# A four-layer graph network on one core: the sort's transposes get a PSUM bank of their own, the second batch's layers have two

## The chip, the cores and the metric

The kernel runs on one core of a Trainium2 chip. The metric is the device time of one execution in microseconds (us), and of several executions the median. A profile is one more execution with the hardware profiler on: it has a span from the first to the last instruction, and a time of its own that is a little longer than the span. The engines are TensorE (PE), VectorE (DVE), ScalarE (ACT), GpSimd (POOL) and SyncE (SP), which issues most of the DMA transfers. ACT issues some transfers too.

## The reference

Sixteen graphs of 1024 nodes and 64 channels go through four layers, each of them x = x + layer(relu(layernorm(x))). Layer 0 drops some edges of each node, sorts the values of the remaining neighbours in each channel, and takes three quantiles:

```
h = jnp.maximum(_layernorm(x, axis=-1), 0.0)
x = x + _L0_gnn_ref(h, adj, nodemask, ...)       # below
...
vals = jnp.where(nd[..., None], x[:, None, :, :], jnp.inf)
s = jnp.sort(vals, axis=2)
...
for tau, w in zip(TAUS, WTS):
    agg = agg + w * (v_lo + frac * (v_hi - v_lo))
out = x + agg
y = relu(out @ W1 + b1) @ W2 + b2
```

Layer 1 multiplies the adjacency matrix by a small network's output and feeds a gated unit. Layer 2 multiplies it by h again. Layer 3 is an attention over the columns of the adjacency matrix with a softmax. All three need the adjacency matrix, transposed, as a matmul operand.

## The kernel before

**Pairs.** The batches are worked off two at a time, `pairs = B // 2`, so there are eight pairs. What is done for one pair:

- `sort_begin` (L692): loads x of the two batches, normalises it, stores h, and transposes it by eight matmuls (L714) into a tile `cur` with one row for each of 2 x 64 channels. ACT copies the result out of PSUM (L717).
- `sort_pair` (L720): a bitonic network of 55 steps on DVE sorts each channel's 1024 values (L729, L736, L737). Each four steps, the comparisons' results go to DRAM (`m_d`, L740, on SP's queue). Then the 55 steps are undone on a code (L753 to L760), which gives each node its rank code. ACT turns the code into f32 (`cf`, L794), eight matmuls transpose it back (L799), ACT copies it out (L800), and it goes to DRAM as `y_d` (L802).
- `prepare` / `neighbours` (L805): loads the adjacency matrix (`a`, L819), transposes it into `a_d` for the layers (L831, L833), and makes the thinned matrix `ndT` (L825, L854 to L881). A last group of matmuls counts the neighbours (L885), read by DVE (L892).
- `weights` and `select` (L907, L1028): `weights` loads `y_d` into `node` and makes the pieces `wt` from it on DVE (L916, L921). `select` multiplies them by `ndT` (L1045) and picks the quantiles (L1055 to L1160). `extras` (L1251) handles the nodes that did not fit.
- `layers` (L1324): the dense part of layer 0 and layers 1 to 3 of one batch. The matmuls write tiles of one PSUM pool, `bank()` (L1339). `adj_block` loads `a_d` on SP's queue (L1402).

**Order.** The loop at L1566 has, for pair pr: select for pr, extras for pr, then the layers of both batches of pr, and beside them `prepare(pr + 1)`, `sort_pair(pr + 1)` and `sort_begin(pr + 2)`. Nobody writes out the order of an engine's instructions. When the program is built, a list scheduler with its own estimates of durations places each instruction as early as its operands and a free buffer allow, and earlier program text goes first. So the steps of a sort fill DVE's gaps wherever their data is ready. At run time each engine follows the order that was made, waits included. Buffers of one name in a pool are handed out in turn.

**PSUM.** A tile of 512 f32 per partition is one bank. In the layers' stage the pool `nbp` has two banks under one name, `pk`, the pool `lb0` three for the first batch of the pair and `lb1` three for the second. That is all eight. `nbp`'s two serve `prepare` (L829, L865, L882) and the sort's two sets of transposes (L712, L797) alike. `select` uses all eight banks itself (`sp`, `sc`), `extras` six beside `nbp`. The sort's SBUF rows (`row4`, L689) have three buffers and live through the whole kernel.

Of the kernel before, what the change touches and what calls it, by code (L numbers as in the profile page):

```python
# [9 lines left out]
F32 = mybir.dt.float32  # L10
# [10 lines left out]
PSUM = bass.MemoryType.PSUM  # L21
DRAM = bass.MemoryType.DRAM

P = 128
# [18 lines left out]
def gnn_stack(ctx, tc, x, adj, nodemask, w, out):  # L43
# [613 lines left out]
    def norm(pool, big, xt, g, name):  # L657

        st = pool.tile([P, g, 6], F32, name=f"{name}_st")
        mv = pool.tile([P, g, 2], F32, name=f"{name}_mv")  # L660
        for t in range(g):
            nc.vector.bn_stats(st[:, t, :], xt[:, t, :])
        for t in range(g):
            nc.vector.bn_aggr(mv[:, t, :], st[:, t, :])
        sd = pool.tile([P, g], F32, name=f"{name}_sd")
        nc.scalar.activation(sd, mv[:, :, 1], AF.Sqrt, bias=eps, scale=1.0)
        rs = pool.tile([P, g], F32, name=f"{name}_rs")
        nc.vector.reciprocal(rs, sd)
        d = big()
        nc.vector.tensor_sub(d, xt, mv[:, :, 0:1].to_broadcast([P, g, C]))  # L670
        h = big()
        nc.vector.scalar_tensor_tensor(
            h, d, 0.0, rs.rearrange("p (g o) -> p g o", o=1).to_broadcast([P, g, C]), op0=ALU.max, op1=ALU.mult
        )
        return h
# [13 lines left out]
    def row4():  # L689
        return so.tile([P, N], F32, name="s4", bufs=3)  # L690

    def sort_begin(pr, nbp):  # L692

        def rows():
            return row4().rearrange("p (g c) -> p g c", c=C)

        xt = rows()
        x4 = xt.rearrange("p (t b) c -> p t b c", b=2)
        for b in range(2):
            nc.sync.dma_start(x4[:, :, b, :], x[pr * 2 + b].rearrange("(t p) c -> p t c", p=P))  # L700
        h = norm(so, rows, xt, NT * 2, "so")
        h4 = h.rearrange("p (t b) c -> p t b c", b=2)
        for b in range(2):
            nc.sync.dma_start(h_d[pr * 2 + b], h4[:, :, b, :])
        more_ = so.tile([P, N], U16, name="code").bitcast(BF16)
        nc.scalar.activation(more_, h.rearrange("p g c -> p (g c)"), AF.Sign)
        more_ = more_.rearrange("p (t b c) -> p t b c", b=2, c=C)
        for b in range(2):
            nc.sync.dma_start(p_d[pr * 2 + b], more_[:, :, b, :])
        cur = row4()  # L710
        for q in range(0, NT, 4):
            ph = nbp.tile([P, 4, P], F32, name="pk")  # L712
            for t in range(4):
                nc.tensor.transpose(  # L714
                    ph[:, t, :], h[:, 2 * (q + t) : 2 * (q + t) + 2, :].rearrange("p b c -> p (b c)"), ident
                )
            nc.scalar.copy(cur[:, q * P : (q + 4) * P], ph.rearrange("p t n -> p (t n)"))  # L717
        return cur

    def sort_pair(pr, cur, nbp):  # L720

        nxt = row4()
        groups = range(0, len(steps), GROUP)
        for k0 in groups:
            swapped = so.tile([P, GROUP, N // 2], U16, name="swapped", bufs=2)
            for k, (size, j) in enumerate(steps[k0 : k0 + GROUP]):
# [11 lines left out]
                cur, nxt = nxt, cur  # L738
# [55 lines left out]
        nc.scalar.mul(cf, code, -4.0)  # L794
        cn = row4().bitcast(F16)[:, :N].rearrange("p (t k) -> p t k", k=P)
        for q in range(0, NT, 4):
            pc = nbp.tile([P, 4, P], F32, name="pk")  # L797
            for t in range(4):
                nc.tensor.transpose(pc[:, t, :], cf[:, (q + t) * P : (q + t + 1) * P], ident)  # L799
            nc.scalar.copy(cn[:, q : q + 4, :], pc)  # L800
# [106 lines left out]
    def weights(b, sb, behind):  # L907

        node = sb.tile([P, NT, 4, C], F16, name="node")
        nc.sync.dma_start(node[:, :, 0, :], y_d[b])
        positive = sb.tile([P, NT, C], BF16, name="positive", bufs=2)
        nc.sync.dma_start(positive, p_d[b])
        for k in range(1, 4):
            nc.vector.tensor_scalar_add(node[:, :, k, :], node[:, :, 0, :], 4.0 * CODE * k)  # L916
        wt = {}
        for g in PIECES:
            wt[g] = sb.tile([P, NT, 8, C], F8, name="wt", bufs=len(PIECES) + 2)
            for k in range(0, 8, 4):  # L920
                nc.vector.tensor_scalar(  # L921
                    wt[g][:, :, k : k + 4, :].bitcast(U8), node, 4.0 * (25 + CODE * (8 * g + k)), 4.0 * 26,
                    op0=ALU.add, op1=ALU.min,
                )
        order = ExitStack()
        rows = w_d[b * C : (b + 1) * C]
        for part, d_, w0, n in ((0, 4, 0, 32), (1, 4, 40, 32), (2, 16, 32, 8)):
            src = rows.rearrange("(q d) w e -> d w q e", d=d_)
            to = vtab[:, part].rearrange("p (q d e) -> p q d e", d=d_, e=24)
            for d in range(d_):  # L930
                if behind is not None:
                    order.enter_context(tc.issue_after(behind))
                    behind = None
                nc.sync.dma_start(to[d : d_ * n : d_, :, d, :], src[d, w0 : w0 + n])
        order.close()
        return wt, positive
# [603 lines left out]
    def prepare(pr, nb, nbp):  # L1540

        made = []
        for i in range(2):
            made.append((
                ndp.tile([P, NT, N], F8, name=f"ndT{i}"), ndp.tile([P, NT, 10], F32, name=f"row10{i}"),
                ndp.tile([P, NT, 3], F32, name=f"qb{i}"),
                ndp.tile([P, NT], F32, name=f"qz{i}"),
            ))
            neighbours(pr * 2 + i, *made[i], nb, nbp)
        return made  # L1550

    def side_pools():
        return (
            tc.tile_pool(reuse_waits="tile", name="nb", bufs=1),
            tc.tile_pool(reuse_waits="tile", name="nbp", bufs=2, space=PSUM),
        )

    pairs = B // 2
    nb_, nbp_ = side_pools()
    with nb_ as nb, nbp_ as nbp:  # L1560
        sort_pair(0, sort_begin(0, nbp), nbp)
        made = prepare(0, nb, nbp)
        if pairs > 1:
            cur = sort_begin(1, nbp)
    taken = None
    for pr in range(pairs):  # L1566
        with tc.tile_pool(reuse_waits="tile", name="keep", bufs=1) as keep:
            aggs = [keep.tile([P, NT, C], F32, name=f"agg{i}") for i in range(2)]
            kept = {
                "flag": [keep.tile([P, NT], U16, name=f"flag{i}") for i in range(2)],  # L1570
                "vx": keep.tile([P, 9], F32, name="vx"),
            }
            with tc.tile_pool(reuse_waits="tile", name="kn", bufs=1) as kn:
                with (
                    tc.tile_pool(reuse_waits="tile", name="sy", bufs=2) as sy,
                    tc.tile_pool(reuse_waits="tile", name="sw", bufs=1) as sw,
                    tc.tile_pool(reuse_waits="tile", name="sg", bufs=2) as sg,
                    tc.tile_pool(reuse_waits="tile", name="sp", bufs=2, space=PSUM) as sp,
                    tc.tile_pool(reuse_waits="tile", name="sc", bufs=2, space=PSUM) as sc,
                ):  # L1580
                    for i in range(2):
                        wt, positive = weights(pr * 2 + i, kn, None if i else taken)
                        select(pr * 2 + i, i, wt, positive, *made[i], aggs[i], kept, sw, sg, sy, sc, sp)
            nb_, nbp_ = side_pools()
            with nb_ as nb, nbp_ as nbp:
                with tc.tile_pool(reuse_waits="tile", name="xs", bufs=1) as xs, tc.tile_pool(reuse_waits="tile", name="xp", bufs=1, space=PSUM) as xp:
                    taken = extras(pr, kept, aggs, xs, xp)
                with (
                    tc.tile_pool(reuse_waits="tile", name="ly0", bufs=1) as ly0,
                    tc.tile_pool(reuse_waits="tile", name="ly1", bufs=1) as ly1,  # L1590
                    tc.tile_pool(reuse_waits="tile", name="lb0", bufs=3, space=PSUM) as lb0,
                    tc.tile_pool(reuse_waits="tile", name="lb1", bufs=3, space=PSUM) as lb1,
                ):
                    for i, (ly, lb) in enumerate(((ly0, lb0), (ly1, lb1))):
                        layers(pr * 2 + i, (pr * 2 + i) % 4, aggs[i], ly, lb)
                    if pr + 1 < pairs:
                        made = prepare(pr + 1, nb, nbp)
                        sort_pair(pr + 1, cur, nbp)
                    if pr + 2 < pairs:
                        cur = sort_begin(pr + 2, nbp)  # L1600
    sorting.close()


# [1 line left out]
    with tc.tile_pool(name="fl", bufs=1) as fl, tc.tile_pool(name="flp", bufs=1, space=PSUM) as flp:  # L1605
        pr = flp.tile([P, P], F32, name="pr")
# [41 lines left out]
```

## Time and profile before

| what | us |
|---|---|
| median of 3 runs (lowest, highest) | 6534.98 (6533.89, 6546.8) |
| the profiled execution, its own time | 6547.95 |
| the profiled execution, its span | 6546.1 |
| select of pair 1, in the profile | 1213.1 to 1674.6 |
| extras of pair 1 | 1674.6 to 1764 |
| layers of pair 1, with what runs beside them | 1764 to 1982.6 |
| select of pair 7, the last | 5828.2 to 6260.7 |
| extras of pair 7 | 6260.7 to 6325.8 |
| layers of pair 7, with nothing beside them | 6325.8 to 6536.3 |

A window of the profile gives, for each engine, the time in which it was busy and the number of its instructions. In a timeline a line is the start, the duration, the engine, the line of the kernel, the operation, what it writes and reads, and in brackets how long the engine had been idle before it and what ended that.

### The profile page before, as it was taken

What the parts mean: (1) busy time and instruction counts of PE and PEld (TensorE: products, weight loads), DVE (VectorE), ACT (ScalarE), POOL (GpSimd) and SP (SyncE); (2) the same over time, 40 slices, a digit from 0 to 9 for tenths busy, and PEclk for the clock granted to TensorE, in tenths of its full rate; (3) what the DMA queues carried; (4) which work ended last, traced back from release to release, by engine and by line L of the source; (5) the groups of instructions that cost most, each with busy time, mean ns of one, the idle gap of its engine ahead of it and who ended that gap; (6) DMA issues with size and microseconds to landing.
All of it is one profiled execution on the core that took longest, in us unless ns stands there. A gap on an engine that the chain in (4) does not pass through costs nothing.

```text
span 6546.1 us, 112888 instructions
## 1 busy us (share of the span) xinstructions
PE 4538.7 (69%) x45010; PEld 2819.2 (43%) x45010; DVE 5301.1 (81%) x13031; ACT 3545.5 (54%) x4348; POOL 137.5 (2%) x234
## 2 busy tenths in 40 slices
PE   0167858777577776778577775777767876777856
PEld 0145544355434544355443554344543544435532
DVE  7759985999769996899959998599977999586645
ACT  0165655556456556565555565555555655555623
POOL 0000000000000000000000000000000000000000
PEclk9978868788688887888788897888878888888967
DMA  1320135211451124401352114611155013520024
GB/s 56 110 72 33 57 106 177 70 42 49 137 176 39 50 89 141 128 35 51 92 187 75 39 52 118 188 48 51 51 157 150 33 59 89 176 70 16 8 69 126
DMA packets 525639, 568.14 MB, mean 87 GB/s; under 512 B 265004, under 2 KB 414894, under 8 KB 525102
## 3 DMA queue, kind: packets, MB, share of 16 engines
q1 hardware_dynamic: 381472, 476.43, 24.1%
q10 hardware_dynamic: 142862, 82.31, 4.1%
q8 instruction: 355, 5.82, 0.4%
q0 software_dynamic: 768, 2.10, 0.2%
q14 instruction: 182, 1.49, 0.1%
HBM read 376.95 MB, written 183.76 MB: 86 GB/s over the span
## 4 chain that ended last, share of the span: by engine, by line
PE 44%; DVE 23%; ACT 18%; DMA 11%; issue 4%; ACTq 0%; SPq 0%; POOL 0%; DVEq 0%; POOLq 0%
PE comb L1045 17%; PE cand L1148 6%; ACT sign L1103 6%; DMA adjT<-a_d 4%; PE comb L1101 4%; PE bank L1409 4%; DVE y L1119 3%; ACT y L1055 2%; PE comb L1236 2%; DMA a<-in_adj_dram 2%; PE pk L875 2%; DVE att L1519 2%; DVE adjT L1513 2%; DVE cand L1156 2%; DMA a_d<-at 1%
## 5 line engine op out<-in xcount | busy, mean ns | idle before, releaser
L1045 PE MATMUL comb<-wt,ndT 128*128 128x512 fp8e5 x6144 | 1518.2, 404 | 60.3 <-DVE top L1516 29.3
L1055 ACT ACTIVATE y<-comb,qb 128x1024 int16<-128x1024 f32 (+1 forms) x640 | 629.9, 1025 | 954.4 <-PE comb L1045 954.3
L1045 PEld LDWEIGHTS <-ndT 128*128 128x128 fp8e5 x6144 | 617.7, 103 | 804.3 <-issue 207.6
L1119 DVE TENSOR_TENSOR y<-y 128x512 uint16<-128x512 uint16 (+5 forms) x896 | 703.9, 790 | 66.5 <-PE comb L1101 50.8
L1148 PE MATMUL cand<-vtab,sign 128*128 128x48 f16 (+1 forms) x18432 | 680.6, 192 | 71.9 <-DVE agg L1018 29.0
L1148 PEld LDWEIGHTS <-sign 128*128 128x128 fp8e5 x18432 | 648.1, 97 | 143.6 <-issue 51.7
L1101 PE MATMUL comb<-ident_b,y 128*128 128x128 bf16 x4608 | 392.1, 255 | 436.2 <-ACT sign L1103 382.9
L1103 ACT ACTIVATE sign<-comb,half 128x2048 fp8e5<-128x2048 int16 (+1 forms) x384 | 591.6, 1541 | 124.1 <-PE comb L1101 112.1
L1103 ACT ACTIVATE sign<-comb,lower 128x2048 fp8e5<-128x2048 int16 (+1 forms) x384 | 590.9, 1539 | 0.0
L1156 DVE COPY_PREDICATED cand<-w_f,cand 128x256 f32<-128x256 uint16 (+1 forms) x1536 | 529.5, 376 | 70.7 <-PE cand L1148 69.1
L1101 PEld LDWEIGHTS <-y 128*128 128x128 bf16 x4608 | 357.9, 115 | 460.2 <-issue 454.0
L825 DVE TENSOR_TENSOR_SCAN cum<-ni 128x1024 f16<-128x1024 fp8e5 x128 | 292.9, 2294 | 149.3 <-ACT sq L854 131.1
L1409 PE MATMUL bank<-adjT,nd 128*64 128x512 f32 x1024 | 309.2, 662 | 97.0 <-DMA adjT<-a_d 91.7
L833 ACT COPY at<-pk 128x512 f32<-128x512 f32 x256 | 146.7, 586 | 334.5 <-DMA a_d<-at 167.6
L1409 PE MATMUL bank<-att,hs 128*64 128x512 f32 x512 | 206.9, 893 | 165.7 <-ACT hs L1524 164.8
L875 PE MATMUL pk<-ident_b,ni 128*128 128x128 bf16 x1024 | 217.8, 239 | 145.5 <-ACT at L833 80.0
L729 DVE TENSOR_TENSOR swapped<-s 128x512 uint16<-128x512 f32 x440 | 302.0, 686 | 12.2 <-DMA m_d<-swapped 3.9
L736 DVE TENSOR_TENSOR s<-s 128x512 f32<-128x512 f32 (+2 forms) x440 | 288.5, 656 | 0.0
L921 DVE TENSOR_SCALAR wt<-node 128x2048 uint8<-128x2048 f16 x224 | 267.6, 1216 | 25.8 <-PE comb L1236 25.7
L737 DVE TENSOR_TENSOR s<-s 128x512 f32<-128x512 f32 (+2 forms) x440 | 288.4, 655 | 0.0
L875 PE MATMUL pk<-minus_b,rem 128*128 128x128 bf16 x1024 | 219.3, 242 | 88.3 <-ACT rem L856 88.3
L760 DVE TENSOR_TENSOR code<-code,xo 128x1024 uint16<-128x1024 uint16 x360 | 264.2, 734 | 4.6
(300 smaller groups left out, 8065.3 us busy)
## 6 DMA issues: line engine op xcount, KB each, us to landing
adjT<-a_d SPq DMA_DIRECT2D x384, 512.0 KB
a<-in_adj_dram SPq DMA_DIRECT2D x128, 512.0 KB
a_d<-at ACTq DMA_DIRECT2D x256, 256.0 KB
m_d<-swapped SPq DMA_DIRECT2D x104, 512.0 KB
swapped<-m_d SPq DMA_DIRECT2D x104, 512.0 KB
n_d<-nat SPq DMA_DIRECT2D x128, 128.0 KB
x_d<-xr SPq DMA_DIRECT2D x48, 256.0 KB
comb_x<-x_d ACTq DMA_DIRECT2D x24, 512.0 KB
```

Source lines behind the costliest of these rows:

```text
L729: nc.vector.tensor_tensor(side(swapped[:, k, :], j), hi, lo, op=ALU.is_gt)
L736: nc.vector.tensor_tensor(to_lo, lo, hi, op=ALU.max)
L825: nc.vector.tensor_tensor_scan(cum[:, t - t0, :], ni[:, t, :], wide[:, t, pad - 1 : pad - 1 + N], 0.0, op0=ALU.add, op1=ALU.add)
L875: nc.tensor.matmul(pk[:, n % 4, :], lhs, rhs, start=(n % 4 == 0 and m == 0), stop=(m == len(terms) - 1 and last),)
L1045: nc.tensor.matmul(pw[:, e, :], ndT[:, j, t * P : (t + 1) * P], piece[:, j].rearrange("p w c -> p (w c)"), start=(j == 0), stop=(j == NT - 1),
L1055: nc.scalar.activation(y[:, 0, chunks, at : at + words_ * d_].rearrange("p q (w d) -> p q w d", d=d_), by_word[:, : words_ * C].rearrange( ...
L1101: nc.tensor.transpose(pt[:, q - q0, :], y[:, 0, q, :].bitcast(BF16), ident_b)
L1103: nc.scalar.activation(signs[tl][s][:, q0:q1, :], pt.bitcast(I16), AF.Sign, bias=before[s], scale=-1.0, saturate=False,)
L1119: nc.vector.tensor_tensor(v[:, :, :, :n], v[:, :, :, :n], v[:, :, :, n : 2 * n], op=ALU.max)
L1148: nc.tensor.matmul(cand[:, e, at : at + 12 * d_].rearrange("p (d l) -> p d l", l=12), signs[tl][sec][:, chunk, :], tab[:, q, :, half_ * 12 ...
L1156: nc.vector.copy_predicated(v[:, :, :, dst : dst + k], mk.to_broadcast([P, 2, C // 2, k]), v[:, :, :, frm : frm + k])
L1409: nc.tensor.matmul(po[to : to + C, :], lhs, rhs[:, f * HALF : (f + 1) * HALF], start=(j == 0), stop=(j == NT - 1))
```

## The change

The sort's transposes no longer take tiles of `nbp`. They take them from a new pool `sop` with one bank, and the name of the tile is `ps`. In the loop that bank is opened beside the layers' pools, so it exists from the end of `extras` to the end of the layers. `lb1` gives up one of its three banks for it. Before the loop `sop` stands beside `nbp`. No instruction is added or taken away.

```
-    def sort_begin(pr, nbp):
+    def sort_begin(pr, sop):
...
-            ph = nbp.tile([P, 4, P], F32, name="pk")
+            ph = sop.tile([P, 4, P], F32, name="ps")
...
-    def sort_pair(pr, cur, nbp):
+    def sort_pair(pr, cur, sop):
...
-            pc = nbp.tile([P, 4, P], F32, name="pk")
+            pc = sop.tile([P, 4, P], F32, name="ps")
...
     with nb_ as nb, nbp_ as nbp:
-        sort_pair(0, sort_begin(0, nbp), nbp)
-        made = prepare(0, nb, nbp)
-        if pairs > 1:
-            cur = sort_begin(1, nbp)
+        with tc.tile_pool(reuse_waits="tile", name="sop", bufs=1, space=PSUM) as sop:
+            sort_pair(0, sort_begin(0, sop), sop)
+            made = prepare(0, nb, nbp)
+            if pairs > 1:
+                cur = sort_begin(1, sop)
...
-                    tc.tile_pool(reuse_waits="tile", name="lb1", bufs=3, space=PSUM) as lb1,
+                    tc.tile_pool(reuse_waits="tile", name="lb1", bufs=2, space=PSUM) as lb1,
+                    tc.tile_pool(reuse_waits="tile", name="sop", bufs=1, space=PSUM) as sop,
...
                         made = prepare(pr + 1, nb, nbp)
-                        sort_pair(pr + 1, cur, nbp)
+                        sort_pair(pr + 1, cur, sop)
                     if pr + 2 < pairs:
-                        cur = sort_begin(pr + 2, nbp)
+                        cur = sort_begin(pr + 2, sop)
```

## The prediction

> **What bounds the kernel now.** I read the page first, for the engines and the chain of work that ended last.
>
> ```profile
> PE 4538.7 (69%) x45010; PEld 2819.2 (43%) x45010; DVE 5301.1 (81%) x13031; ACT 3545.5 (54%) x4348; POOL 137.5 (2%) x234
> PE 44%; DVE 23%; ACT 18%; DMA 11%; issue 4%; ACTq 0%; SPq 0%; POOL 0%; DVEq 0%; POOLq 0%
> ```
>
> DVE is the busiest, yet PE leads the chain: no single engine bounds the kernel, so each stage has to be read by itself. Next I read the timeline where the sort's transposes stand, in the layers of pair 0.
>
> ```profile
> 974.37 1.04 ACT L794 ACTIVATE s<-code 128x1024 f32<-128x1024 uint16 x1
> ...
> 1139.37 1.74 PE L885 MATMUL pk<-ones_b,ndT 128*128 128x1 bf16 x64 [0.18 <-ACT ndT L881]
> 1140.97 0.64 PE L799 MATMUL pk<-ident,s 128*128 128x128 f32 x4
> ...
> 1188.47 1.97 PE L714 MATMUL pk<-ident,s 128*128 128x128 f32 x8 [3.49 <-DVE s L672]
> ```
>
> The code is ready at 975.4, but its transpose runs at 1141, right behind `prepare`'s last matmuls (L885): it takes its turn for a `pk` tile. `sort_begin` of the pair after next follows it, so its DVE work falls after 1150, and the next sort starts at 1217. Before the loop it is the same: `sort_begin`'s h is ready at 303.7, and its L714 runs at 426.39.
>
> Third, windows of these stretches (columns: PE, PEld, DVE, ACT, POOL busy; granted clock; DMA share and GB/s).
>
> ```profile
> 1020.00:1140.00 120.00, 102.10 (x553) 49.55 (x554) 59.20 (x188) 72.61 (x107) 5.15 (x9) 0.87 0.59 186
> 1140.00:1213.00 73.00, 43.48 (x178) 16.10 (x175) 71.72 (x160) 31.79 (x45) 0.00 (x0) 0.67 0.40 106
> 305.00:428.00 123.00, 68.64 (x625) 55.47 (x625) 40.68 (x72) 81.05 (x113) 5.16 (x11) 0.62 0.37 106
> 1213.10:1674.60 461.50, 356.41 (x4074) 233.00 (x4073) 434.25 (x1073) 267.37 (x315) 4.18 (x7) 0.88 0.17 52
> 5828.20:6260.70 432.50, 345.05 (x4030) 226.09 (x4028) 280.08 (x756) 258.88 (x299) 2.03 (x2) 0.88 0.07 19
> ```
>
> While `prepare` runs, DVE is half idle (60.8 of 120 us). After it, DVE is full (71.7 of 73), with `sort_begin`'s work in it. The last two lines are a natural experiment: pair 7's select has no sort in its DVE gaps, and 154 us less DVE work makes it only 29 us shorter than pair 1's.
>
> **What the Trainium skill says.** "PSUM — Partial Sum Buffer", its specifications: 8 banks per partition of 512 f32 each, so a bank for the sort must come from another pool. The trace shows no banks, but the pools' sizes add up to eight. The same page, "Engine vs sequencer instructions": ScalarE's, VectorE's and GpSimd's queues are strict FIFO, and matmuls start in program order. The trace agrees: at 1188.47 PE had idled 3.49 us for the sort's L672. "Perfetto Trace Analysis", "Optimization Strategy": regimes with different busiest engines may gain by being interleaved. That is what happens here if sort steps move out of the full select into the half-empty layers. "DMA: Bandwidth & Descriptors", "Issuing engines are not separate DMA queues": all issuers share the same 16 DMA engines, and the 0.59 share between 1020 and 1140 is all of them together.
>
> **The change part by part.** The sum is made against the profiled execution, 6547.95 us, span 6546.1. The median of the runs, 6534.98, is 13 us lower, and I take that off at the end.
>
> (1) *The tail of the layers, six stages (pairs 0 to 5; no sort_begin follows later).* The code's transposes can run once `extras` has left its PSUM, about 1000 instead of 1141. Then y_d, the load of x, the normalisation and L714 follow, and leave the full stretch. `sort_begin`'s DVE work is 6.4 us: 2.7 for 16 statistics, 1.1 for 16 aggregates, 1.2 + 1.2 + 0.2. What this is worth shows in pair 6's layers, which have none: counted in the timeline, an eighth of the next pair's L1045 matmuls is done 21.1 us after the layers' end (the last L1532), against 25.3 to 27.0 for pairs 1 to 6. I take 5.5 us a stage: -33.
>
> (2) *The same work in the middle.* DVE's cover is its 60.8 idle us. But L714 is moved past `prepare`'s and the layers' matmuls on PE, and PE will wait there for L672 again (3.5 us). ACT takes two copies (0.57 each), one Sign (1.04), one Sqrt (0.3) and up to two table loads (1.28 each) with 72.6 of 120 us busy. On SP, y_d, x, h_d and p_d, eight transfers, stand among the loads of `adjT`. None of these is fully exposed: 0 to 6 us a stage, I take 2: +12.
>
> (3) *Sort steps into the layers.* With `cur` ready at about 1035, DVE has some 45 us of gaps left until 1140. Up to 22 of the sort's 55 steps (0.686 + 0.656 + 0.655 = 2.0 us each) fit. The planner doesn't see the real gaps, so I take 15 steps, 30 us; bounds are 0 and 45. In select and extras as many vanish. Price in select: 460.5 (mean of pairs 1 to 6) less 432.5 is 28; less the 5.5 of (1) is 22.5 us for 175.8 us of sort steps (L729 to L760 summed over a select), 0.128 a us. Price in extras: pair 7's take 65.1 us, the others' 89; the difference of 24 comes from 19.6 us of sort steps and from `prepare`, whose DVE work there is as long, so I take half of 24/19.6 at most, and of that half again: 0.3. The sort ends earlier, so extras lose their 19.6 us first: 19.6 x 0.3 + 10.4 x 0.128 = 7.2. Against it, in the layers DVE is late for the layers' own work: at 0.15 a us, between the two prices, 4.5. Net -2.7 a stage: -16.
>
> (4) *Before the loop.* L714 comes at about 304 instead of 426. DVE has 82 idle us until 428. I take 37 steps, 75 us, out of select 0 at 0.128: -9.6; the fillers and nine stores of `m_d` cost `prepare` 3: -7.
>
> (5) *Two banks for lb1, eight stages.* Most of a batch's tiles are a chain in which each waits for the one before. Only the four gate tiles (L1459, L1464, L1466, L1467) and the three tiles around L1395 and L1503 use three at a time. A bank came free 2.7 us after the group before in pair 0 (1084.30 to 1086.96). With three banks one gate tile waits, with two banks two. So 0 to 2.7 us, beside adjT loads that often end last: I take 1.5 a stage: +12.
>
> (6) *`nbp` without the sort.* The sort's four tiles a stage are out of its turn, two of them at its end: nothing is queued behind them but the next stage's first L1045, and that waits for L921 on DVE. Nothing, with (1) counted.
>
> Sum: -33 + 12 - 16 - 7 + 12 = -32. From 6548 that is 6516, less 13 is 6503. Since the terms that I chose freely, (2) and (3), are more likely too good than too bad, I set the forecast at 6510, -0.4%.
>
> **Rivals.**
> (R1, slower) *SP's queue.* Sort steps in the layers bring their `m_d` stores with them, at the head of an in-order queue that also feeds `adjT`.
>
> ```profile
> SPq L740 <- DVE swapped L729: 429.2, 59, 27.4
> SPq L1402 <- PE bank L1409: 409.4, 210, 26.6
> ```
>
> SP stood 7.3 us (429.2/59) at such a store in select, where little is queued behind it. In the layers the loads of `adjT`, two buffers deep, stand behind: in 985 to 1145 the chain spends 21.8% on adjT's landing. Four stores a stage at half of 7.3 us in six stages are 88 us: 6510 + 88 is about 6600. It decides from some 9 us a stage on (then (1), (3) and (4) are eaten up). For it: the layers alone (pair 7) take 210.5 us, with `prepare` beside 216 to 224, so they are a chain of waits. Against it: SP is seldom far ahead.
> (R2, larger gain) *The gaps are filled wholly*, all 45 us in each stage, and the layers don't feel it: another 15 x 0.128 + 4.5 = 6.4 us a stage, and (2) at nothing: 6510 - 38 - 12 = 6460.
> (R3, no change) *The tail's gain is used up*: DVE's work is the same in total, the gaps are the planner's and not real, and (1) is balanced by (2) and (5): 6535. Part of it is that the change doesn't do what it says, L799 being held by something else than `pk`; against that stands the seven-fold sight of L799 right behind L885.
>
> **How the numbers follow.** Forecast 6510 (6480 to 6522): 0.38. R2: 0.10. R3: 0.15. R1: 0.37, from 6548 up, since a static order that is remade everywhere can also be worse in places that I can't see. About 0.2% (13 us) is what a measurement of this kernel can tell from no change. So faster 0.48, same 0.15, slower 0.37. The forecast's own range is 6480 to 6522; for 8 in 10 I leave out half of R2 and a quarter of R1: 6455 to 6620. The bounds of (2), (3) and (5) (36, 40 and 22 us) lie inside.
>
> **What would show it.** Right: L799 at about 1000 in pair 0 and L714 before 1050; sort steps (L729) before 1213; L714 at about 304 before the loop; DVE between 1020 and 1140 busy over 90 us; the last L753 before the end of select. Wrong: layers that end later after extras than now (216 to 224 us), with adjT's landings or SP behind L740 as what ended the waits (R1); or L799 still behind L885 (R3).

## The result and the profile after

The changed kernel takes 6484.55 us (median of 4 runs, 6477.07 to 6491.56); the kernel before, run beside it, 6536.67 (4 runs, 6533.89 to 6546.8). The ratio is 0.9917, with a 95% interval of 0.99 to 0.9934: faster by 0.8%, where the forecast was 0.4%. The time lies inside the stated range, but the gain is twice as large and, as will be seen, comes from another place. The profiled execution has 6477.07 us and a span of 6475.2, which is 70.9 below the span of before.

The page after, first the engines, then the busy tenths of PE and the chain that ended last:

```profile
PE 4545.8 (70%) x45010; PEld 2849.6 (44%) x45010; DVE 5339.2 (82%) x13031; ACT 3530.8 (55%) x4337; POOL 138.4 (2%) x234
...
PE   3177766776777858678577776777766776778856
...
PE 36%; DVE 33%; ACT 13%; DMA 10%; issue 7%; SPq 1%; POOL 0%; ACTq 0%; DVEq 0%; POOLq 0%
```

And the busy tenths of PE in the kernel before:

```profile
PE   0167858777577776778577775777767876777856
```

The work of each engine is the same to 1%. The chain has moved from PE (44% before) to DVE (33%, 23% before). What differs to the eye is the left end of PE's row: a slice is some 163 us, and PE is idle in the first one before and not after.

The timeline of PE in the layers of pair 0, after:

```profile
902.10 1.75 PE L885 MATMUL pk<-ones_b,ndT 128*128 128x1 bf16 x64 [0.18 <-ACT ndT L881]
...
908.81 0.60 PE L799 MATMUL ps<-ident,s 128*128 128x128 f32 x4
...
916.19 1.06 PE L799 MATMUL ps<-ident,s 128*128 128x128 f32 x4
...
957.28 0.61 PE L714 MATMUL ps<-ident,s 128*128 128x128 f32 x4
...
973.33 0.60 PE L714 MATMUL ps<-ident,s 128*128 128x128 f32 x4
...
1046.96 1.74 PE L885 MATMUL pk<-ones_b,ndT 128*128 128x1 bf16 x64 [0.18 <-ACT ndT L881]
```

Here the change does what it says. `prepare` counts neighbours (L885) once for each of the pair's two batches, here at 902 and at 1047. The code's transposes (L799) run at 909, long before the second of these groups and not behind it. `sort_begin`'s (L714) follow in the middle of the layers, 154 us before these end at 1127.2. The windows after, for the middle and the tail of pair 0's layers and for select of pair 1 (columns as in the prediction):

```profile
934.00:1054.00 120.00, 97.18 (x582) 46.65 (x581) 93.00 (x265) 73.68 (x109) 6.00 (x9) 0.91 0.67 212
1054.00:1127.00 73.00, 42.83 (x152) 14.39 (x151) 72.31 (x129) 29.24 (x42) 0.00 (x0) 0.75 0.28 84
1127.20:1588.00 460.80, 352.63 (x4044) 231.24 (x4043) 414.90 (x1055) 264.94 (x311) 3.95 (x7) 0.87 0.16 48
```

The first two windows lie as far from the layers' end as those of the prediction. DVE is busy for 93 of 120 us where it was busy for 59, and in select for 415 us where it was 434. So the sort's steps did move. But select is as long as before (460.8 against 461.5 us).

**By stage.** I take as marks the last L1148 (end of select), the last L1306 (end of extras) and the last L1532 (end of the layers), all from the timeline, and give means over pairs 1 to 5 in us:

| kernel | select | extras | layers | together | sort steps in the layers |
|---|---|---|---|---|---|
| before | 461.2 | 89.2 | 220.2 | 770.7 | 0 |
| after | 454.9 | 87.2 | 234.0 | 776.0 | 41.0 |

In the loop the change costs 5.3 us a pair (worked out before rounding): select and extras gain 8.3, the layers lose 13.8. The gain must lie ahead of the loop. There the first L1045 of pair 0's select starts at 434.3 before and at 339.2 after, 95 us earlier. From there on pair 0 takes 9 us more, pairs 1 to 5 take 27 more together, pair 6 takes 2 less, pair 7 takes 8 less and the end 2 less: -95 + 24 = -71, which is the difference of the spans.

**What lies before the loop.** PE's waits in the first 330 us, before (columns: us in total, times, longest):

```profile
PE pk L799 <- ACT s L794: 206.4, 1, 206.4
PE pk L714 <- DVE s L672: 66.9, 1, 66.9
```

And PE's timeline, before:

```profile
280.38 1.97 PE L799 MATMUL pk<-ident,s 128*128 128x128 f32 x8 [206.36 <-ACT s L794]
282.17 3.99 PE L831 MATMUL pk<-ident,a 128*128 128x128 f32 x16
```

PE stands for 206 us at the first sort's code transposes, until the sort is finished. The next instruction in its queue, 1.8 us later, is `prepare`'s first transpose (L831). The program text names the sort first, so its tiles of `pk` come first in turn, and all of `prepare(0)` waits for a sort that it doesn't need. The windows of before show what this costs:

```profile
0.00:282.00 282.00, 4.04 (x17) 3.32 (x17) 228.26 (x484) 10.66 (x17) 5.45 (x15) 1.00 0.22 68
282.00:428.00 146.00, 77.85 (x666) 61.65 (x664) 53.00 (x107) 92.75 (x130) 6.81 (x15) 0.64 0.42 122
```

First DVE works and PE doesn't (4 of 282 us), then PE and ACT work and DVE is idle for 93 of 146 us. After, the windows are:

```profile
0.00:212.00 212.00, 80.79 (x653) 65.12 (x654) 165.04 (x336) 95.40 (x130) 22.80 (x30) 0.69 0.38 118
212.00:330.00 118.00, 2.37 (x26) 1.78 (x23) 108.71 (x252) 6.96 (x12) 0.00 (x0) 0.51 0.30 89
```

And PE's timeline, after:

```profile
210.71 1.74 PE L885 MATMUL pk<-ones_b,ndT 128*128 128x1 bf16 x64
327.40 1.12 PE L799 MATMUL ps<-ident,s 128*128 128x128 f32 x4 [114.95 <-ACT s L794]
...
336.00 1.09 PE L714 MATMUL ps<-ident,s 128*128 128x128 f32 x4 [5.69 <-DVE s L672]
...
339.17 6.05 PE L1045 MATMUL comb<-wt,ndT 128*128 128x512 fp8e5 x17 [0.29 <-DVE wt L921]
```

`prepare(0)` has its last matmuls at 211 instead of 425, beside the sort. PE still waits 115 us for the sort, but nothing is queued behind it that could run. The sort itself ends 47 us later (L799 at 327.4, where it was 280.4), since its steps now share DVE with `prepare`. DVE's work is nearly the same (228.3 + 53.0 = 281.3 us before, up to 428; 165.0 + 108.7 = 273.7 after, up to 330), but it is now done without the gap of 93 us. My reading is that this gap is the gain; the experiments below test it.

### The profile page after: what moved, and what is told of

The parts are those of the page before. It is cut to its first block, busy times and chain, and to the rows that moved or that the text cites. A ratio compares the mean times of both kernels' runs of the same rounds, so it can differ in the third digit from the quotient of the medians.

```text
span 6475.2 us, 112886 instructions
## 1 busy us (share of the span) xinstructions
PE 4545.8 (70%) x45010; PEld 2849.6 (44%) x45010; DVE 5339.2 (82%) x13031; ACT 3530.8 (55%) x4337; POOL 138.4 (2%) x234
## 4 chain that ended last, share of the span: by engine, by line
PE 36%; DVE 33%; ACT 13%; DMA 10%; issue 7%; SPq 1%; POOL 0%; ACTq 0%; DVEq 0%; POOLq 0%
PE comb L1045 13%; PE cand L1148 6%; ACT sign L1103 5%; DMA adjT<-a_d 4%; DVE y L1119 4%; PE comb L1101 3%; PE bank L1409 3%; PE comb L1236 2%; DVE att L1519 2%; DVE cand L1156 2%; DVE cum L825 2%; DMA a<-in_adj_dram 2%; DVE code L760 2%; DVE adjT L1513 2%; ACT y L1055 2%
## 5 line engine op out<-in xcount | busy, mean ns | idle before, releaser
L1045 PE MATMUL comb<-wt,ndT 128*128 128x512 fp8e5 x6144 | 1503.0, 401 | 26.1 <-DVE top L1516 11.1
L1045 PEld LDWEIGHTS <-ndT 128*128 128x128 fp8e5 x6144 | 615.3, 103 | 794.4 <-issue 188.5
L1148 PE MATMUL cand<-vtab,sign 128*128 128x48 f16 (+1 forms) x18432 | 701.9, 194 | 105.1 <-DVE agg L1018 53.7
L1148 PEld LDWEIGHTS <-sign 128*128 128x128 fp8e5 x18432 | 668.0, 98 | 174.9 <-issue 76.8
L921 DVE TENSOR_SCALAR wt<-node 128x2048 uint8<-128x2048 f16 x224 | 269.3, 1217 | 23.6 <-PE comb L1236 23.5
```

Source lines behind the costliest of these rows:

```text
L1045: nc.tensor.matmul(pw[:, e, :], ndT[:, j, t * P : (t + 1) * P], piece[:, j].rearrange("p w c -> p (w c)"), start=(j == 0), stop=(j == NT - 1),
L1148: nc.tensor.matmul(cand[:, e, at : at + 12 * d_].rearrange("p (d l) -> p d l", l=12), signs[tl][sec][:, chunk, :], tab[:, q, :, half_ * 12 ...
```

## The experiments

My theory A after the result was: the gain lies before the loop, and the loop's part costs. The rivals were that the loop gains as forecast, or that the second batch's banks matter. Nine kernels took these apart. The stages, as above, in us; "prepare(0) ends" is the start of its last L892:

| kernel | median | ratio (95%) | prepare(0) ends | end of pair 0's layers | select | extras | layers |
|---|---|---|---|---|---|---|---|
| before | | | 426.6 | 1213.1 | 461.2 | 89.2 | 220.2 |
| after | 6484.55 | 0.9917 (0.99 to 0.9934) | 212.5 | 1127.2 | 454.9 | 87.2 | 234.0 |
| ahead of the loop alone | 6444.86 | 0.9844 (0.983 to 0.9857) | 212.8 | 1114.0 | 461.0 | 89.4 | 219.6 |
| loop alone | 6599.33 | 1.0084 (1.0071 to 1.0097) | 426.3 | 1227.5 | 455.5 | 86.2 | 236.3 |
| no sort steps in the layers | 6450.99 | 0.986 (0.9845 to 0.9874) | 213.3 | 1117.1 | 458.5 | 87.9 | 226.6 |
| lb1 with two banks alone | 6550.24 | 1.0007 (1.0 to 1.0015) | 426.8 | 1214.6 | 457.1 | 91.0 | 221.4 |
| other order of the text alone | 6450.89 | 0.9866 (0.9851 to 0.9881) | 234.7 | 1125.8 | 460.1 | 88.4 | 219.8 |
| sort_begin back on pk in the loop | 6423.37 | 0.9826 (0.9812 to 0.9839) | 213.4 | 1120.2 | 459.6 | 87.1 | 219.1 |
| no early stores of m_d | 6470.74 | 0.99 (0.9885 to 0.9915) | 211.4 | 1125.1 | 459.6 | 86.6 | 227.3 |
| first code's bank alone | 6437.25 | 0.9841 (0.9826 to 0.9856) | 278.5 | 1110.5 | 461.8 | 89.6 | 219.2 |
| ahead of the loop, lb1 with two | 6438.65 | 0.985 (0.9831 to 0.9869) | 212.0 | 1119.0 | 457.3 | 89.0 | 220.0 |

Each ratio is against runs of the kernel before on the same chip, whose medians were 6536.67 (for the change), 6543.31, 6540.82 and 6538.6. The stages are read from one profile of each kernel. Pair 0's first L1045 starts at 434 in the three kernels whose first code waits in the turn ahead of `prepare` (before, the loop alone, `lb1` alone), and between 334 and 348 in all the others.

### Ahead of the loop alone, and the loop alone

From before, with the bank's name handed to both functions as `nm`. Ahead of the loop alone (the new lines):

```
+        with tc.tile_pool(reuse_waits="tile", name="sop", bufs=1, space=PSUM) as sop:
+            sort_pair(0, sort_begin(0, sop, "ps"), sop, "ps")
+            made = prepare(0, nb, nbp)
+            if pairs > 1:
+                cur = sort_begin(1, sop, "ps")
...
+                        sort_pair(pr + 1, cur, nbp, "pk")
...
+                        cur = sort_begin(pr + 2, nbp, "pk")
```

> The change before the loop alone; in the loop the sort keeps the pk tiles and lb1 its three banks. Theory A (the gain is before the loop: there the first prepare stood behind the first sort's code transposes for its turn at pk): the first select starts some 95 us earlier, as in the changed kernel, and the loop is as before, so 6536 - 86 to 95: 6440 to 6450, faster than the changed kernel. Rival B (the gain is made in the loop, before it only the 7 us that the prediction gave it): about 6530.

Measured: 6444.86, which is 1.56% or about 100 us under before, and 40 us under the full change. The stages of the loop are those of before.

The loop alone:

```
-        sort_pair(0, sort_begin(0, nbp), nbp)
+        sort_pair(0, sort_begin(0, nbp, "pk"), nbp, "pk")
...
-                    tc.tile_pool(reuse_waits="tile", name="lb1", bufs=3, space=PSUM) as lb1,
+                    tc.tile_pool(reuse_waits="tile", name="lb1", bufs=2, space=PSUM) as lb1,
+                    tc.tile_pool(reuse_waits="tile", name="sop", bufs=1, space=PSUM) as sop,
...
+                        sort_pair(pr + 1, cur, sop, "ps")
...
+                        cur = sort_begin(pr + 2, sop, "ps")
```

> The change in the loop alone; before the loop as it was. Theory A: the layers with the sort's steps beside them are about 14 us longer a pair, select and extras about 9 us shorter, so in all 5 to 20 us slower: 6540 to 6555. Rival B: it holds the gain, about 6490.

Measured: 6599.33, some 55 us over before, and more than I had expected. The layers are longer by 16 us. So the change is a gain of some 100 and a loss of some 55 in one. The sum, 0.9844 + 0.0084 = 0.9928, lies within the interval of the change's own ratio. The rival that the loop gains falls.

### The turn for the bank, or the number of banks

If the turn at `pk` is the cause, another order of the text without any new bank must do the same:

```
-        sort_pair(0, sort_begin(0, nbp), nbp)
+        cur0 = sort_begin(0, nbp)
         made = prepare(0, nb, nbp)
+        sort_pair(0, cur0, nbp)
```

> The kernel before, all pools as they were; before the loop the text calls sort_begin(0), then prepare(0), then sort_pair(0), so that the code's transposes take their turn at pk behind prepare's and not ahead of them. Theory A (it was the turn at pk, not the number of banks): prepare runs beside the sort and the time is 6440 to 6470. Rival (a bank more was needed): 6530 or more.

Measured: 6450.89, nearly the whole of the gain with the pools of before. PE's timeline in this kernel:

```profile
232.84 1.85 PE L885 MATMUL pk<-ones_b,ndT 128*128 128x1 bf16 x64
332.89 1.97 PE L799 MATMUL pk<-ident,s 128*128 128x128 f32 x8 [98.21 <-ACT s L794]
```

The code's transposes are still in `pk`, but behind `prepare`. Then the opposite cut: all as before, text order too, but the two transpose groups of the first code (not `sort_begin`'s) in their own bank (the new lines):

```
+        with tc.tile_pool(reuse_waits="tile", name="sop", bufs=1, space=PSUM) as sop:
+            sort_pair(0, sort_begin(0, nbp, "pk"), sop, "ps")
+            made = prepare(0, nb, nbp)
+            if pairs > 1:
+                cur = sort_begin(1, nbp, "pk")
```

> The kernel before with one difference: the first sort's two code transposes (L799 before the loop) take a bank of their own; everything else, both sort_begin before the loop too, stays on pk. Theory A: all of the gain is there, 6440 to 6450. Rival (sort_begin's transposes count too): above 6480.

Measured: 6437.25; its interval and that of the change ahead of the loop cover each other. PE's waits in its first 330 us:

```profile
PE pk L875 <- ACT rem L856: 86.6, 14, 24.2
PE pk L714 <- DVE s L672: 66.7, 1, 66.7
```

PE still stands 66.7 us for the first `sort_begin`, so `prepare` starts at 74 and ends at 278 instead of 212, and this costs nothing: pair 0's layers end at 1110.5, the earliest of all. In its first 279 us DVE is busy for 228. Until the first L1045, DVE is idle for 147 us in before, and for 58 to 68 us here, with the other order of the text, and in the change: the difference is most of the 95 us. So the end of `prepare` did not matter here; that DVE need not idle while it runs did. These two runs settle the cause of the gain: the turn of the first code's transposes ahead of `prepare`'s, not the number of banks and not `sort_begin`'s turn.

### What the loop's part costs

Sort steps out of the layers, all else as after. The instructions of `sort_pair(pr + 1)` may only be placed behind `held`, the first piece of `wt` (L921) of pair pr. That is made for pair pr's select, so the sort can't begin in the layers ahead of it:

```
-                        sort_pair(pr + 1, cur, sop)
+                        with tc.issue_after(held):
+                            sort_pair(pr + 1, cur, sop)
```

> The changed kernel, with the steps of the next sort held on DVE behind the first piece of weights (L921) of the pair beside whose select they ran before, so that none runs in the layers; sort_begin stays early and lb1 has two banks. Theory C (the 41 us of sort steps in a pair's layers are what makes the layers 14 us longer): the layers of pairs 1 to 5 go back from 232-236 to 218-222 us, select and extras get 5 to 9 us longer, in all about 25 to 40 us faster than the changed kernel, 6445 to 6460. Rival D (it is sort_begin's work in the middle, or the second batch's two banks): the layers stay above 230 us, and the time is 6485 or more.

Measured: 6450.99, and 226.6 us of layers. The sort steps in the layers fell from 41.0 to 2.0 us. So of the 13.8 us that the layers lost, 7.4 belong to the sort's steps, and 6.4 stay without them. I had looked for more. The other side of the trade shows too: select and extras are 4.3 us longer than after (3.6 and 0.7). So 39 us of sort steps cost the layers 7.4 and gave 4.3 elsewhere.

Next, `sort_begin` back to the end, with the code's transposes still in their own bank:

```
-                        cur = sort_begin(pr + 2, sop)
+                        cur = sort_begin(pr + 2, nbp, "pk")
```

> The changed kernel, but in the loop sort_begin takes its tiles from pk again, so it comes late, and no sort step can run in the layers; the code's transposes keep the bank sop, lb1 two banks. Theory (of the 14 us a pair that the changed kernel's layers are longer, 7 are the sort's steps, and the other 7 are sort_begin's work in the middle): layers of pairs 1 to 5 at 218 to 222 us, time as with the change before the loop alone, 6435 to 6450. Rival (the 7 us come from the early code transposes or the second batch's two banks): layers at 226 to 229, about 6465.

Measured: 6423.37, the fastest of all: faster than both kernels, and by the medians than the change ahead of the loop alone (their intervals, 0.9812 to 0.9839 and 0.983 to 0.9857, still touch). Without an early `cur` hardly any of the sort runs in the layers either (2.7 us). The layers are at 219.1, as before. So the other half of the loss comes with `sort_begin` in the middle, and not with the early code transposes or `lb1`'s two banks, which this version has as well. The windows of pair 4's layers, after:

```profile
3999.70:4233.10 233.40, 170.47 (x1013) 85.83 (x1008) 191.14 (x451) 121.02 (x180) 9.91 (x15) 0.83 0.54 169
```

without sort steps in the layers:

```profile
3984.50:4210.10 225.60, 171.39 (x998) 81.33 (x993) 154.48 (x388) 115.83 (x173) 8.94 (x15) 0.83 0.53 164
```

and with `sort_begin` late:

```profile
3968.30:4183.30 215.00, 165.02 (x978) 80.78 (x973) 153.71 (x387) 115.86 (x172) 8.95 (x15) 0.85 0.54 171
```

Between the second and the third, the busy times of DVE and ACT and the DMA share are alike (PE's is 6.4 us longer, at a clock of 0.83 for 0.85). Over pairs 1 to 5 the mean clock of the layers is 0.84 in both versions, so the clock isn't the cause. The same work takes 10.6 us longer here, and 7.5 on the mean of five pairs; what the two versions differ in is where `sort_begin` stands. Which piece of it does this (x's load and the stores on SP, ACT's copies, PE's wait at L714) was not tried.

Two banks for `lb1`, and nothing else:

```
-                    tc.tile_pool(reuse_waits="tile", name="lb1", bufs=3, space=PSUM) as lb1,
+                    tc.tile_pool(reuse_waits="tile", name="lb1", bufs=2, space=PSUM) as lb1,
```

> The kernel before with lb1 at two banks and nothing else (one bank idle). The prediction's term: 12 us slower, 6549. Theory now, since the last two pairs' layers were no longer in the changed kernel: within 5 us of before, 6532 to 6542.

Measured: 6550.24, above what I had expected, but before gave 6543.31 on the same chip: a ratio of 1.0007 (1.0 to 1.0015), so 0 to 10 us for the whole kernel. The layers are 1.2 us longer, select 4 us shorter, extras 1.8 us longer.

The stores that the moved steps bring to SP (R1): after, without the stores of the first five groups to `m_d`. This leaves out part of the computation: the undoing of the sort reads the sixth group's comparisons in place of those of the first five. A flag's threshold at L1613 is raised so that the kernel stays out of its other branch.

```
-            nc.sync.dma_start(m_d[k0 // GROUP, :, :n], swapped[:, :n])
+            if k0 >= 5 * GROUP:
+                nc.sync.dma_start(m_d[k0 // GROUP, :, :n], swapped[:, :n])
...
-            nc.sync.dma_start(swapped[:, :n], m_d[k0 // GROUP, :, :n])
+            nc.sync.dma_start(swapped[:, :n], m_d[max(k0 // GROUP, 5), :, :n])
```

> The changed kernel without the stores to m_d of each sort's first five groups of four steps, which are those that run in the layers; the loads of these groups read another group's slot instead, and the fallback for overfull cases is switched off, so part of the result is left out. Theory R1 (SP's queue: the stores hold up adjT's loads): the layers of pairs 1 to 5 lose most of the 7 us that the sort's steps cost, 226 to 229 us, about 6450. Rival (DVE itself is late for the layers' own work): they stay at 232 to 235 us, about 6480.

Measured: 6470.74, between the two expectations, and its interval overlaps that of the change. The layers fall from 234.0 to 227.3, but select rises from 454.9 to 459.6: some 2.5 us a pair are left. The waits of SP's queue in pair 1's layers, after:

```profile
SPq L1402 <- DVE att L1519: 51.9, 8, 16.4
SPq L1402 <- PE bank L1409: 40.1, 26, 6.1
...
SPq L740 <- DVE swapped L729: 4.8, 3, 2.3
```

in before:

```profile
SPq L1402 <- DVE att L1519: 20.4, 6, 8.0
```

and without the early stores, where the lines of the code are one higher:

```profile
SPq L1403 <- DVE att L1520: 55.9, 9, 11.0
SPq L1403 <- PE bank L1410: 40.4, 25, 3.6
```

The loads of `adjT` wait for DVE as long without the stores as with them, and at the stores themselves SP stands for 4.8 us. So the layers are shorter without the stores, but the waits don't show that SP's order is how. Nor does the longer wait than in before (20.4 us) mark the loss: with `sort_begin` late it is 46.7 us on the mean of pairs 1 to 5, and those layers are as short as before. How the layers lose their time stays open.

### Where the last 20 us come from

The fastest version is 21 us below the change ahead of the loop alone by the medians, taken on two chips, and some 12 by the ratios; since the intervals touch, the difference isn't sure. Is it `lb1`, or the early y_d? To the version with the change ahead of the loop alone:

```
-                    tc.tile_pool(reuse_waits="tile", name="lb1", bufs=3, space=PSUM) as lb1,
+                    tc.tile_pool(reuse_waits="tile", name="lb1", bufs=2, space=PSUM) as lb1,
```

> The kernel with the change before the loop only, and beside it two banks for lb1; in the loop the sort's transposes all stay on pk, and the freed bank is used by nobody. It asks where the 20 us come from by which the version with sort_begin on pk and the code's transposes in their own bank (6423) is below the change before the loop alone (6445). Theory A (they come from lb1's two banks, whose one run by itself on the kernel before could not see them): 6420 to 6430, extras near 87 and pair 7's layers near 204. Theory B (they come from the code's transposes being free of prepare, so that y_d and the next pair's weights are early): 6440 to 6450, extras near 89.4; pair 7's layers, where no sort runs, may be near 204 all the same.

Measured: 6438.65, with an interval (0.9831 to 0.9869) that reaches into that of both others. Extras, at 89.0, speak for theory B: they are below 88 only in the kernels whose code transposes are free of `prepare` in the loop. But in pairs 1 to 5 together the two versions are alike (766.3 and 765.8 us). The question stays open.

## Why the prediction was right in sign and wrong in size

**Step (4) failed.** It put -7 on what lies before the loop; alone, that part gave about -100. I had read L714 at 426 behind h at 303.7, and asked what held up the sort. I didn't ask the question the other way round: what does the sort hold up when its turn comes first? So the term took `prepare(0)`'s place, behind the first sort, as given, and that was what the change undid. I had even noted the 82 idle us of DVE until 428, and saw in them room for sort 1, not a hole made by the first sort. The mechanism I named did not occur at all: L714 of pair 1 runs at 336.0, not 304, and sort 1 starts with select 0 as it did before. L714 waits there for h from DVE, which was busy for 108.7 of the 118 us from 212 to 330; that this fullness made h late is likely, but wasn't tested. That the total came inside the stated range was luck: a gain that I hadn't seen met a loop whose sign I had wrong. The first slice of the page's rows had hinted at it: PE at 0 tenths in the first slice. The passage that I took from the Trainium skill ("PSUM — Partial Sum Buffer", "Engine vs sequencer instructions": matmuls start in program order) was what was needed. I applied it to a wait of 3.49 us, where the trace of before had one of 206.4 us.

**Step (1), the tail**, was right in its mechanism. L1045 of the next pair starts 41 us before the layers' end, where it was 17, and an eighth of its matmuls is reached 8 us sooner after that end (5.5 forecast). Since the end itself comes later, none of it is left over.

**Step (2), sort_begin in the middle**, was mis-sized: I took 2 us of a range up to 6; the layers with an early `sort_begin` and no sort steps are 6.4 us longer than before, and 7.5 longer than with it late.

**Step (3), the sort's steps in the layers**, was mis-sized on both sides, and so had the wrong sign. Its cost was 4.5 us for 30 us of steps, against 7.4 for 39 (0.19 a us, with 0.15 taken). Its gain was 7.2 us for 30 (0.24 a us), against 4.3 for 39 (0.11 a us). All that select and extras gain is 8.3 us a pair, in which the tail of (1) is contained; together I had forecast 12.7. With (5), I had made the four terms of the loop -25. By the spans they are +24. By the medians they are some +43, as the profiled run of before lies 11 us above its median and that of after 7 below. The loop alone measures +55.

**Step (5), two banks for lb1**, was too dear: 0 to 10 us measured alone for 12. **Step (6)**, nothing, is not contradicted by any run.

**The rivals.** R1 put 9 us a stage as the point from which the loop would turn the sign. The layers did lose 13.8, so the loop by itself is R1's case in its sign. But its place was only partly right: leaving out the stores gives back 6.7 us in the layers and takes 4.7 in select. R3's remark that the gaps "are the planner's and not real" comes closest to the loop: DVE's busy time in the layers rose from 147 to 191 us, and the layers grew by a third of that. What would have shown it, of my list: DVE at 93 of 120 us, sort steps before the layers' end and L799 long before L885 all came true, and still did not mean a gain. Of the signs of being wrong, the longer layers came true as well (234 us, where 216 to 224 was the mark).

## What to carry to other kernels

Where two independent streams take buffers of one name in turn, look in the waits for one very long wait of an in-order engine, and ask what is queued behind it that does not need it: here one wait of 206 us was followed by 93 us of idle DVE, and a change in the order of a few lines of text gives nearly all of it back. Cut a change into its places and run each alone before you explain the sum: here a gain of 100 and a loss of 55 looked like a small success. And filler work in the gaps of a stage that is a chain of waits isn't free; here the layers paid 0.19 us for each us of it, and the stages that gave it up gained 0.11.

## What the runs showed that I had not expected

`sort_begin`, 6.4 us of DVE work with a few transfers and copies, makes the layers some 7 us longer in their middle, where DVE was idle half of the time, than at their end, where DVE is full; why is open. And a stage that is full of DVE work (228 of the first 279 us, with the first code's bank alone) can contain all of `prepare` at no cost that these runs can tell, though `prepare` then ends 66 us later.
